# A decoder on one core: the first scan step's inputs in another order, a token shift by transfers, a later turn to tokens

## The chip, the core and the metric

The kernel runs on one core of a Trainium2 chip. A core has five engines with an instruction stream each: TensorE (PE, whose weight loads the profile shows as PEld), VectorE (DVE), ScalarE (ACT), GpSimd (POOL) and SyncE (SP, which issues most transfers here). They work on a common on-chip memory, TensorE writes its results into PSUM, and semaphores order the streams. Within one stream instructions run in the order in which they stand. The metric is the device time of one execution in microseconds.

## The reference

The input `x` is 4 sequences of 512 tokens with 128 features, in float32; a context of 32 tokens for each sequence serves two cross attentions. Six blocks follow each other, each as `x = layernorm(x + block(x))`:

```
x = _layernorm(x + _L0_attn_ref(x, ...))    # selective scan (Mamba), 256 channels, 16 states
x = _layernorm(x + _L0_xattn_ref(x, ...))   # cross attention, 16 heads, gated
x = _layernorm(x + _L0_ffn_ref(x, ...))     # shared + 8 experts, 2 of them for each token
x = _layernorm(x + _L1_attn_ref(x, ...))    # banded self attention, 16 heads of 8
x = _layernorm(x + _L1_xattn_ref(x, ...))   # cross attention, 16 heads
x = _layernorm(x + _L1_ffn_ref(x, ...))     # two layers: local attention, gated feed-forward
```

Three places matter here. In the scan block each sequence goes through a projection, a convolution over four tokens, `silu`, and projections that give `delta = softplus(...)`, `B` and `C`; then `h = exp(delta * A) * h + delta * B * u` runs over the tokens for each of the 16 states, and the result is multiplied by `silu(z)`. In the last block each layer has

```
def shift_token(t):
    t1, t2 = jnp.split(t, 2, axis=-1)
    t2 = jnp.pad(t2, ((0, 0), (1, 0), (0, 0)))[:, :-1]
    return jnp.concatenate([t1, t2], axis=-1)
```

before the attention and again before the feed-forward part: features 64 to 127 come from the token before. After the second shift a layernorm is taken over the features of each token.

## The kernel before

Tokens lie on the 128 partitions, four tiles of 128 tokens a sequence; `T` is 512, `NJ` 4, `B` 4, `NT` 16. All stages stand one after the other in one program. In the parts that matter the order on each engine is written out by hand (`tc.manual_schedule()`): functions are called in the order in which their instructions are to stand in the streams, and the framework adds the waits.

**Front of the scan (L356 to L400).** For sequence 0: squares and their sums give `inv`, the tokens are scaled and turned to features (`xnp`), and the two halves `c` of the 256 channels are projected and convolved, half 0 by four accumulating matmuls with `w_tap` (L375), half 1 by one projection and four DVE instructions (L370, L372) into `acc`. `squares_` of the sequences 1 to 3 stand ahead of that, on ACT and DVE, and `inverses` ahead of half 0's convolution. After the silus (L376, L377), `double` projects to `px` (three copies of B and C, and the step's rank), `rests` takes what bfloat16 drops, `gates` and two silus make `sz`, `steps_` computes softplus in passes `t`, `v`, `w` on ACT, `corrected` and `reduced` mend its rounding, `logarithms` takes the log, `deltas` and `products` give `delta` and `du` (half 0 on POOL, half 1 on DVE), and `parts` completes `stk`, the bfloat16 pieces of B and C.

**The scan (L563 to L598).** 64 steps, state by state for each sequence. Step `k`: `rows` spreads a row of B and one of C over the partitions with a selecting matmul from `stk` (`pb`, `pc`, copied by ACT to `cb`), `decay` makes `dA` on ACT three steps ahead, `scan` multiplies `pb` by `du` (L432), runs the scan (L435) on DVE and multiplies by `cb` on POOL (L440), `collect` sums up on PE. The table `ahead` prepares the next sequence in the gaps; `gates_next` ends with two silus of 1024 columns (L548). `gated` (L450) uses `sz` of a sequence one sequence later.

**Banded attention (L1335 to L1360).** 64 steps `s`, four to a tile `i` of 128 queries. Each step: `scores(s + 1)` (matmuls into `psc`, then the maximum `nm` on DVE), `exponentials(s + 1)` on ACT, `weights(s)` (eight transposes `ptp` and copies to `pT`, one by DVE and one by ACT), `values(s - 1)`. What follows a finished tile is spread over the next steps by

```
tail = [[None, gathered], [by_tokens, None], [by_features, output], [normed, None]]
```

with the first entry of a pair right after `scores` and the second after `values`. `gathered` copies `pa` to `ao` on ACT, `by_tokens` turns it with four transposes `pn` and divides on DVE. `made` prepares the next sequence. `pn`, `pq`, `pto` and `po` share the one buffer of a PSUM tag.

**Last block (L1731 to L1792).** A loop over `g`, two to each tile `i` (four heads each), eight half blocks `q` (two layers, four sequences). `around` and `feed` say which function stands in which of three places of a step; `feed` lags one or two half blocks behind. `output` writes `xa`; `ff_shift` turns `xa` to features (`shifted`: four transposes `pts`, an ACT copy and a DVE copy by one column), one step later `ff_tokens` turns it back (`pth`, ACT copy to `hn`), the step after `ff_stats` takes means and variances, then `ff_norm`, `ff_features`, `ff_gates`, `ff_hidden`, `ff_out`. Functions ask PSUM for buffers of the tag `pt`, of which there are three. `project_v` copies values to `va` and sends them by transfers on SP to `vh`, shifted by 64 partitions. After the loop the last half block (`e`) runs alone.

Of the kernel before, what the change touches and what calls it, by code (L numbers as in the profile page):

```python
# [11 lines left out]
F32 = mybir.dt.float32  # L12
# [45 lines left out]
def decoder_kernel(ctx: ExitStack, tc: tile.TileContext, a: dict):  # L58
# [34 lines left out]
    def vcol(name, i=0):  # L93
        o = _VEC[name][0] + i
        return vec[:, o:o + 1]
# [141 lines left out]
    with ExitStack() as ph:  # L237
# [30 lines left out]
        def squares_(b):  # L268
            sq = fp.tile([P, T], F32, tag="left", name="sq", bufs=1)
            sq = sq.rearrange("p (j d) -> p j d", d=D)  # L270
            S.activation(sq, x0[:, b * NJ:(b + 1) * NJ, :], AF.Square)
            V.tensor_reduce(inv[:, b], sq, AX.X, ALU.add)

        def inverses(lo, hi):
            t = inv[:, lo:hi].rearrange("p b j -> p (b j)")
            V.tensor_scalar(t, t, 1.0 / D, 1e-5, ALU.mult, ALU.add)
            rpow(t, t, (hi - lo) * NJ)
# [17 lines left out]
        def gates(b, c, pi):  # L295
            mm(pi, w_in[:, (2 + c) * P:(3 + c) * P], xnp[:, 3:])
# [18 lines left out]
            G.tensor_tensor(stk[64:96, b, :], left[64:96], mid[64:96], ALU.subtract)  # L315


        def steps_(b, c, pd):
            mm(pd, w_dt[96:104, c * P:(c + 1) * P], xdts[b][96:104])
            t = fp.tile([P, T], F32, tag="e", name="e")  # L320
            v = fp.tile([P, T], F32, tag="v", name="v")
            S.activation(t, pd, AF.Abs, bias=vcol("dt_b", c))
            S.activation(v, pd, AF.Relu, bias=vcol("dt_b", c))
            S.activation(t, t, AF.Exp, scale=-1.0)
            w = fp.tile([P, T], F32, tag="w", name="w")
            S.activation(w, t, AF.Identity, bias=1.0)
            evs[b, c] = t, v, w

        def corrected(b, c):
# [25 lines left out]
        with tc.tile_pool(name="m1ps", bufs=1, space=PSUM) as ps, tc.manual_schedule():  # L355
            squares_(0)  # L356
            inverses(0, 1)
            xns[0] = fp.tile([P, NJ, D], F32, tag="e", name="xn")
            V.tensor_tensor(xns[0], x0[:, 0:NJ, :], inv[:, 0].unsqueeze(2).to_broadcast([P, NJ, D]), ALU.mult)
            by_features(0, ps.tile([P, NJ, P], F32, tag="pt", name="pt"))  # L360
            for c in range(2):
                G.tensor_tensor(w_tap[:, c], w_tap[:, c],
                                w_in[:, c * P:(c + 1) * P].unsqueeze(1).to_broadcast([P, 4, P]), ALU.mult)
            for b in range(1, B):
                squares_(b)

            pi = ps.tile([P, T], F32, tag="pi1", name="pi")
            mm(pi, w_in[:, P:2 * P], xnp[:, 3:])
            acc = u[:, 1, 0, :]
            V.tensor_scalar(acc, pi, vcol("conv_w", 7), vcol("conv_b", 1), ALU.mult, ALU.add)  # L370
            for k in range(1, 4):
                V.scalar_tensor_tensor(acc[:, k:], pi[:, 0:T - k], vcol("conv_w", 7 - k), acc[:, k:], ALU.mult, ALU.add)  # L372
            inverses(1, B)
            pi = ps.tile([P, T], F32, tag="pi0", name="pi")
            convolved(0, 0, pi, range(4))  # L375
            S.activation(u[:, 1, 0, :], acc, AF.Silu)  # L376
            S.activation(u[:, 0, 0, :], pi, AF.Silu, bias=vcol("conv_b", 0))  # L377
            double(0, ps.tile([104, T], F32, tag="px", name="px"))
            rests(0)
            pz = [ps.tile([P, T], F32, tag=f"pz{c}", name="pz") for c in range(2)]  # L380
            for c in range(2):
                gates(0, c, pz[c])
                S.activation(sz[:, c, 0, :], pz[c], AF.Silu)
            S.activation(gate, rcol("gate"), AF.Tanh)
            pct = ps.tile([P, P], F32, tag="pi1", name="pct")
            TE.transpose(pct, ctx_sb, ident)
            V.tensor_copy(ctxT, pct)
            a0 = _VEC["A_log"][0]
            S.activation(negA, vec[:, a0:a0 + 32], AF.Exp)
            V.tensor_scalar_mul(negA, negA, -1.0)  # L390
            V.tensor_scalar_mul(gb, rcol("b_out"), gate)
            for c in range(2):
                steps_(0, c, ps.tile([P, T], F32, tag=f"pd{c}", name="pd"))
                corrected(0, c)
                reduced(0, c, (G, V)[c])
            logarithms(0)
            for c, eng in ((0, G), (1, V)):
                deltas(0, c, eng)
                products(0, c, eng)
            parts(0)  # L400


        with tc.tile_pool(name="m2", bufs=3) as t2, \
# [19 lines left out]

            def decay(k):
                b, n = steps[k]
                for c in range(2):
                    S.activation(dAs[k % 4][:, c, c:T], delta[b % 2][:, c, c:T], AF.Exp,  # L427
                                 scale=negA[:, c * NST + n:c * NST + n + 1])

# [112 lines left out]
            def gates_next(b, c):  # L542
                pi = bank()
                gates(b, c, pi)
                S.copy(sz[:, c, b, :], pi)
                if c:
                    for t in (u, sz):
                        S.activation(t[:, :, b, :], t[:, :, b, :], AF.Silu)  # L548

            def double_next(b):  # L550
                double(b, bank()[0:104])
# [605 lines left out]
    with tc.tile_pool(name="wa", bufs=2) as bp, tc.tile_pool(name="wa_p", bufs=2) as t1, \  # L1157
# [150 lines left out]
        def normed(i):  # L1308
# [4 lines left out]
        made = {3: [(turn_x,)], 5: [(rotary, 0, 0)], 6: [(rotary, 0, 1)], 7: [(rotary, 1, 0)], 9: [(rotary, 1, 1)],  # L1313
                10: [(head_values,)], 11: [(head_keys, 0), (head_keys, 1)], 12: [(head_keys, 2), (head_keys, 3)],
                13: [(head_keys, 4), (head_keys, 5)], 14: [(head_keys, 6), (head_keys, 7)]}
        tail = [[None, gathered], [by_tokens, None], [by_features, output], [normed, None]]

        def tails(s, k):
            i = s // 4 - 1
# [4 lines left out]
        with tc.manual_schedule():  # L1324
            beside = {3: [(blocks_x, 1)], 5: [(g_x, 0)], 6: [(g_x, 1)], 7: [(g_x, 2)], 9: [(g_x, 3)], 10: [(v_x, 0), (v_x, 1)],
                      11: [(v_x, 2)], 12: [(v_x, 3)]}
            blocks_x(0)
            for t in sorted(made):
                for f, *c in made[t]:
                    f(0, *c)  # L1330
                for f, *c in beside.get(t, []):
                    f(*c)
            scores(0)
            exponentials(0)
            last = 4 * NT  # L1335
            for s in range(last):
                if s + 1 < last:
                    scores(s + 1)
                tails(s, 0)
                if s + 1 < last:  # L1340
                    exponentials(s + 1)
                weights(s)

                if s < HT_:
                    for q in range(2):
                        gather(1, 2 * s + q)
                if s % 2 == 0 and 4 <= s < 4 + 2 * HT_:
                    combined(1, s // 2 - 2)
                if s % 2 and 4 <= s < 4 + 2 * HT_:
                    norm_3(1, s // 2 - 2)  # L1350
                if s:
                    values(s - 1)
                tails(s, 1)
                if s // 16 + 1 < B:
                    for f, *c in made.get(s % 16, []):
                        f(s // 16 + 1, *c)
            values(last - 1)
            for s in range(last, last + 4):
                tails(s, 0)
                tails(s, 1)  # L1360

    kept.close()

# [27 lines left out]
    with tc.tile_pool(name="la_b", bufs=2) as bp, tc.tile_pool(name="la_t", bufs=2) as t1, \  # L1391
# [1 line left out]
            tc.tile_pool(name="la_ps", bufs=2, space=PSUM) as ps:  # L1393


        hTz = [bp.tile([P, T], F32, tag=f"hT{k}", name=f"hT{k}", bufs=1) for k in range(3)]
        for k in hTz:
            V.memset(k[64:128, 0:1], 0.0)
        va = bp.tile([P, NJ, 8, 65], F32, tag="va", name="va", bufs=1)
# [5 lines left out]
        ins = [x5]  # L1405
        hTs, pqks, tas, tbs, rns, sss, qTs, pes, pTs, ats, aTs = ({} for _ in range(11))
        xTs, xes, xps, xpTs = ({} for _ in range(4))
        xas, h2s, hns, hnTs, xabs, ges, mvs, fins = ({} for _ in range(8))


        def shift(b):
# [149 lines left out]
            V.tensor_tensor(xas[i // NJ][:, i % NJ, :], po, ins[i // NT][:, i % NT, :], ALU.add)  # L1561

        def ff_shift(q):
            l, b = divmod(q, B)
            xa = xas.pop(q)
            h2s[q] = hTz[2]
            shifted(nc, ps, xa, 0, h2s[q], ident, 3)
            xabs[q] = bp.tile([P, NJ, D], F32, tag="xab", name="xab", bufs=2)
            G.tensor_tensor(xabs[q], xa,
                            rcol("f_b2", 128 * l, 128).unsqueeze(1).to_broadcast([P, NJ, D]), ALU.add)  # L1570
            if l == 1:
                G.tensor_tensor(xabs[q], xabs[q], x5[:, b * NJ:(b + 1) * NJ, :], ALU.add)

        def ff_tokens(q):
            pt = ps.tile([P, NJ, P], F32, tag="pt", name="pth", bufs=3)
            hT = h2s.pop(q)
            for j in range(NJ):
                TE.transpose(pt[:, j, :], hT[:, j * P:(j + 1) * P], ident)
            hns[q] = bp.tile([P, NJ, D], F32, tag="hn", name="hn", bufs=1)
            S.copy(hns[q], pt)  # L1580

        def ff_stats(q):
            mv, rs = stats4(hns[q])
# [114 lines left out]
        def x_norm(b):  # L1698
# [14 lines left out]

        feed = {(0, 0): [[], [], [(ff_hidden, 2, 0)]], (0, 1): [[], [(ff_hidden, 2, 1)], []],
                (1, 0): [[(ff_shift, 1)], [(ff_hidden, 2, 2)], []],
                (1, 1): [[(ff_tokens, 1)], [], []],
                (2, 0): [[(ff_stats, 1)], [(ff_out, 2)], []],
                (2, 1): [[], [], [(ff_norm, 1)]],
                (3, 0): [[(last_stats, 2)], [], []],
# [11 lines left out]
        with tc.manual_schedule():  # L1731
# [46 lines left out]
            ff_shift(e)  # L1778
            for c in range(3):
                ff_hidden(e - 1, c)  # L1780
            ff_tokens(e)
            ff_stats(e)
            ff_out(e - 1)
            ff_norm(e)
# [149 lines left out]
```

## Time and profile before

| | before |
|---|---|
| median of 3 runs | 1281.07 us (1275.3 to 1281.63) |
| profiled execution | 1280.2 us, span 1278.5 us |
| granted TensorE clock, mean | 0.943 |
| busy of the span | PE 86%, DVE 71%, ACT 57%, POOL 50% |
| front, to 38 us | PE 15.5, DVE 13.5, ACT 23.0, POOL 16.9 us busy |
| scan, 38 to 308 us | PE 229, DVE 241, ACT 188, POOL 189 us busy |
| banded attention, 555 to 800 us | PE 217, DVE 165, ACT 140, POOL 43 us busy |
| end, 1230 to 1279 us | PE 31.6, DVE 17.9, ACT 16.6, POOL 8.2 us busy |

A row of the order of time gives start, duration, engine, line and operation, the tiles `out<-in`, the shape and the count; in brackets stands how long the engine was idle before it and which instruction ended that. Rows with a count above 1 are merged, so their duration covers all of them with the gaps. Matmul ends are modelled: the distance between the starts of two groups is TensorE's pitch, and the shown duration of a group is longer than that. L157 and L189 are helpers (`rpow`, `mm`), so their rows are told apart by their tiles.

### The profile page before, as it was taken

The page shows a single profiled execution, that of the slowest core. Times are in us where ns is not written, and L with a number is a line of the kernel's source. Part 1 is how long each engine was busy: PE and PEld are TensorE (multiplying, and loading weights), DVE is VectorE, ACT ScalarE, POOL GpSimd, SP SyncE. Part 2 cuts the span into 40 slices and gives each one's busy share as a digit, 9 for nine tenths or more (in the row PEclk, how much of TensorE's full clock was granted, in tenths as well). Part 3 has the DMA queues.
Part 4 walks back from the last instruction along what each step waited for, and adds up shares of the span by engine and source line. Part 5 has one row for each costly group of instructions (what it writes and reads, how often), then busy time and mean ns, then how long its engine had stood idle before and what let it go on. Part 6 is the DMA issues. An engine that isn't in the chain of part 4 may idle for free.

```text
span 1278.5 us, 22122 instructions
## 1 busy us (share of the span) xinstructions
PE 1100.2 (86%) x8429; PEld 712.8 (56%) x8429; DVE 910.4 (71%) x1722; ACT 729.9 (57%) x1612; POOL 638.2 (50%) x509
## 2 busy tenths in 40 slices
PE   4879888787698789988898998778999999999985
PEld 1334433343366779855555565446666566666563
DVE  3889898897876556847866666687777667766743
ACT  5696958662353445544656565346676665665752
POOL 3568675864546143433110100467785666676621
PEclk9799989897798899989999999899999999999997
DMA  9000000001200612200000000000110100110100
GB/s 270 1 0 1 1 0 1 1 0 65 84 1 30 228 63 80 63 22 14 2 1 2 2 2 2 0 9 21 28 23 14 27 22 15 26 23 14 35 14 17
DMA packets 34573, 38.92 MB, mean 30 GB/s; under 512 B 3378, under 2 KB 25667, under 8 KB 33987
## 3 DMA queue, kind: packets, MB, share of 16 engines
q1 hardware_dynamic: 31874, 31.69, 8.6%
q0 software_dynamic: 2048, 4.20, 1.1%
q10 hardware_dynamic: 544, 1.62, 0.5%
q8 instruction: 66, 1.08, 0.4%
q14 instruction: 41, 0.33, 0.1%
HBM read 20.80 MB, written 9.18 MB: 23 GB/s over the span
## 4 chain that ended last, share of the span: by engine, by line
PE 49%; DVE 16%; ACT 6%; issue 2%; POOL 2%; DMA 0%; DVEq 0%; ACTq 0%; POOLq 0%; SPq 0%
PE psc L189 9%; PE pa L189 4%; PE pqk L189 4%; PE pff L189 3%; PE po L189 3%; PE ptp L1260 3%; PE phg L189 3%; PE pog L189 2%; PE pv L189 2%; PE pof L189 2%; PE ptp L1527 1%; ACT pe L1250 1%; PE ptq L1476 1%; PE pq L189 1%; DVE nm L1243 1%
## 5 line engine op out<-in xcount | busy, mean ns | idle before, releaser
L440 POOL TENSOR_TENSOR h<-h,cb 128x1024 f32<-128x1024 f32 (+1 forms) x65 | 151.8, 2338 | 66.3 <-DVE h L435 49.8
L157 POOL TENSOR_TENSOR rs<-ve,cneg 128x1 f32<-128x1 f32 (+1 forms) x81 | 59.0, 728 | 232.5 <-DVE ve L166 193.8
L435 DVE TENSOR_TENSOR_SCAN h<-dA,pb 128x1024 f32<-128x1024 f32 x64 | 146.4, 2287 | 18.5 <-ACT dA L427 4.9
L1250 ACT ACTIVATE pe<-psc,nm 128x256 f32<-128x256 f32 (+1 forms) x256 | 93.6, 449 | 73.1 <-DVE nm L1243 72.8
L189 PE MATMUL y<-h,ident 128*128 128x512 f32 x256 | 127.2, 620 | 5.4 <-POOL h L440 4.7
L1458 POOL TENSOR_TENSOR ta<-ta,tb 128x1024 f32<-128x1024 f32 x32 | 75.4, 2357 | 111.6 <-DVE rc L1542 65.1
L1243 DVE TENSOR_REDUCE nm<-psc 128x4 f32<-128x1024 f32 (+1 forms) x64 | 69.8, 1091 | 56.7 <-PE psc L189 49.8
L157 POOL TENSOR_TENSOR rn<-ss,cneg 128x16 f32<-128x16 f32 x32 | 93.0, 2906 | 0.0
L1512 DVE TENSOR_REDUCE nm<-psc 128x4 f32<-128x512 f32 x64 | 44.0, 687 | 64.4 <-PE psc L189 62.7
L427 ACT ACTIVATE dA<-delta,negA 128x512 f32<-128x512 f32 (+1 forms) x128 | 85.3, 715 | 4.7 <-POOL delta L346 4.4
L189 PEld LDWEIGHTS y<-h,ident 128*128 128x128 f32 x256 | 49.6, 198 | 65.1 <-issue 46.5
L929 ACT ACTIVATE hTg<-phg,bias 128x128 f32<-128x128 f32 x184 | 52.7, 368 | 57.9 <-PE phg L189 57.2
L432 DVE TENSOR_TENSOR pb<-du,pb 128x1024 f32<-128x1024 f32 x64 | 77.5, 1211 | 2.7 <-PE pb L189 2.2
L1521 ACT ACTIVATE pe<-psc,nm 128x128 f32<-128x128 f32 x256 | 73.8, 381 | 5.4 <-DVE nm L1512 5.3
L189 PE MATMUL pb<-stk,sel 96*128 96x512 bf16 x128 | 41.5, 408 | 32.7 <-DVE h L435 15.5
L1260 PE MATMUL ptp<-ident,pe 128*128 128x128 f32 x448 | 64.5, 281 | 4.8 <-ACT pT L1262 2.0
L189 PE MATMUL pqk<-f_qkv,hT 128*128 128x512 f32 x128 | 64.9, 631 | 4.1 <-DVE tb L1452 4.0
L189 PE MATMUL psc<-kb,qk 64*128 64x256 f32 (+1 forms) x512 | 67.1, 381 | 0.0
L1466 POOL TENSOR_TENSOR ta<-ta,rn 128x1024 f32<-128x1024 f32 x32 | 60.9, 1903 | 2.4
L1260 PEld LDWEIGHTS ptp<-ident,pe 128*128 128x128 f32 x448 | 49.8, 142 | 16.9 <-issue 6.7
L189 PEld LDWEIGHTS <-sel 96*128 96x128 bf16 x192 | 18.9, 103 | 69.3 <-issue 42.3
L1432 ACT ACTIVATE sq<-pqk 128x1024 f32<-128x1024 f32 x32 | 32.9, 1029 | 42.8 <-PE pqk L189 35.3
(375 smaller groups left out, 2879.6 us busy)
## 6 DMA issues: line engine op xcount, KB each, us to landing
vh<-va SPq DMA_DIRECT2D x56, 130.0 KB, 2.3
w<-in_e_w_dram SPq DMA_DIRECT2D x16, 256.0 KB, 5.2
xs<-zero SPq DMA_DIRECT2D x2, 1472.0 KB, 12.7
xg<-xs SPq DMA_DIRECT2D x10, 256.0 KB, 3.1
ys<-yg SPq DMA_DIRECT2D x10, 256.0 KB, 2.4
f_qkv<-in_f_qkv_dram SPq DMA_DIRECT2D x1, 1536.0 KB, 6.6
x<-in_x_dram SPq DMA_DIRECT2D x4, 256.0 KB, 10.8
w_kv<-in_w_kv_dram SPq DMA_DIRECT2D x1, 1024.0 KB, 8.1
```

Of the source, the lines that this page charges most:

```text
L157: G.tensor_tensor(out, in_, cneg.to_broadcast([P, n]), ALU.pow)
L189: TE.matmul(out, lhsT=lhsT, rhs=rhs, start=start, stop=stop)
L427: S.activation(dAs[k % 4][:, c, c:T], delta[b % 2][:, c, c:T], AF.Exp, scale=negA[:, c * NST + n:c * NST + n + 1])
L432: V.tensor_tensor(pb, du[steps[k][0] % 2], pb, ALU.mult)
L435: V.tensor_tensor_scan(h.rearrange("p c t -> p (c t)"), dAs[k % 4].rearrange("p c t -> p (c t)"), pb.rearrange("p c t -> p (c t)"), 0.0, A ...
L440: G.tensor_tensor(h[:, c], h[:, c], cb.unsqueeze(1).to_broadcast([P, n, T]), ALU.mult)
L1243: V.tensor_reduce(nm, psc[:, :, 0:nk], AX.X, ALU.max, negate=True)
L1250: S.activation(pe[:, h, 0:nk], psc[:, h, 0:nk], AF.Exp, bias=nm[:, h:h + 1])
L1260: TE.transpose(ptp[:, h * nb + kk, :], pe[:, 2 * pr + h, kk * P:(kk + 1) * P], ident)
L1458: G.tensor_tensor(ta, ta, tbs.pop(i).rearrange("p w h d -> p (w h) d"), ALU.add)
L1466: G.tensor_tensor(ta, ta, rns.pop(i).unsqueeze(2).to_broadcast([P, 16, 64]), ALU.mult)
L1521: S.activation(pes[g][:, h, :], o[:, par, q, :], AF.Exp, bias=nm[:, k:k + 1])
```

## The change

Four edits. In the front the squares of sequences 1 to 3 move behind the silus of sequence 0; the two passes `v` and `w` of softplus go to DVE; the pieces of `stk` are made right after `px`, two of them on DVE; the gates' projections are copied raw, and their silu is taken in the scan with sequence 1's. `decay` of step 0 takes half 1 ahead of half 0. In banded attention `by_tokens` stands behind `weights` of its step. In the last block `ff_shift` writes `hn` directly: features 0 to 63 by an ACT copy, features 64 to 127 by two transfers on SP that move each token's half to the next partition, and a memset for the first token; `ff_tokens` and the buffer `hT2` go, and `hn` has two buffers.

```diff
-        def steps_(b, c, pd):
+        def steps_(b, c, pd, eng=None):
...
             S.activation(t, pd, AF.Abs, bias=vcol("dt_b", c))
-            S.activation(v, pd, AF.Relu, bias=vcol("dt_b", c))
+            if eng:
+                eng.tensor_scalar(v, pd, vcol("dt_b", c), 0.0, ALU.add, ALU.max)
+            else:
+                S.activation(v, pd, AF.Relu, bias=vcol("dt_b", c))
             S.activation(t, t, AF.Exp, scale=-1.0)
             w = fp.tile([P, T], F32, tag="w", name="w")
-            S.activation(w, t, AF.Identity, bias=1.0)
+            if eng:
+                eng.tensor_scalar_add(w, t, 1.0)
+            else:
+                S.activation(w, t, AF.Identity, bias=1.0)
...
-            for b in range(1, B):
-                squares_(b)
...
-            inverses(1, B)
             pi = ps.tile([P, T], F32, tag="pi0", name="pi")
             convolved(0, 0, pi, range(4))
+            squares_(1)
             S.activation(u[:, 1, 0, :], acc, AF.Silu)
             S.activation(u[:, 0, 0, :], pi, AF.Silu, bias=vcol("conv_b", 0))
+            squares_(2)
+            squares_(3)
+            inverses(1, B)
             double(0, ps.tile([104, T], F32, tag="px", name="px"))
-            rests(0)
-            pz = [ps.tile([P, T], F32, tag=f"pz{c}", name="pz") for c in range(2)]
-            for c in range(2):
-                gates(0, c, pz[c])
-                S.activation(sz[:, c, 0, :], pz[c], AF.Silu)
+            left = fp.tile([P, T], F32, tag="left", name="left", bufs=1)[0:96]
+            V.tensor_tensor(left, xdts[0][0:96], stk[:, 0, :], ALU.subtract)
+            mid = fp.tile([96, T], BF16, tag="mid", name="mid", bufs=1)
+            V.tensor_copy(mid[64:96], left[64:96])
+            V.tensor_copy(stk[32:64, 0, :], left[32:64])
+            G.tensor_tensor(stk[64:96, 0, :], left[64:96], mid[64:96], ALU.subtract)
...
             for c in range(2):
-                steps_(0, c, ps.tile([P, T], F32, tag=f"pd{c}", name="pd"))
+                steps_(0, c, ps.tile([P, T], F32, tag=f"pd{c}", name="pd"), V)
                 corrected(0, c)
                 reduced(0, c, (G, V)[c])
+            for c in range(2):
+                pz = ps.tile([P, T], F32, tag=f"pz{c}", name="pz")
+                gates(0, c, pz)
+                V.tensor_copy(sz[:, c, 0, :], pz)
             logarithms(0)
             for c, eng in ((0, G), (1, V)):
                 deltas(0, c, eng)
                 products(0, c, eng)
-            parts(0)
...
             def decay(k):
                 b, n = steps[k]
-                for c in range(2):
+                for c in range(2) if k else (1, 0):
...
                 if c:
-                    for t in (u, sz):
-                        S.activation(t[:, :, b, :], t[:, :, b, :], AF.Silu)
+                    for t, i in ((u, b), (sz, b)) + ((sz, 0),) * (b == 1):
+                        S.activation(t[:, :, i, :], t[:, :, i, :], AF.Silu)
...
-        tail = [[None, gathered], [by_tokens, None], [by_features, output], [normed, None]]
+        tail = [[None, None, gathered], [None, by_tokens, None], [by_features, None, output], [normed, None, None]]
...
                 weights(s)
+                tails(s, 1)
...
                     values(s - 1)
-                tails(s, 1)
+                tails(s, 2)
...
         def ff_shift(q):
+
             l, b = divmod(q, B)
             xa = xas.pop(q)
-            h2s[q] = hTz[2]
-            shifted(nc, ps, xa, 0, h2s[q], ident, 3)
+            hn = hns[q] = bp.tile([P, NJ, D], F32, tag="hn", name="hn", bufs=2)
+            nc.sync.dma_start(hn[1:P, :, 64:D], xa[0:P - 1, :, 64:D])
+            nc.sync.dma_start(hn[0:1, 1:NJ, 64:D], xa[P - 1:P, 0:NJ - 1, 64:D])
+            G.memset(hn[0:1, 0, 64:D], 0.0)
+            S.copy(hn[:, :, 0:64], xa[:, :, 0:64])
...
-        def ff_tokens(q):
-            pt = ps.tile([P, NJ, P], F32, tag="pt", name="pth", bufs=3)
-            hT = h2s.pop(q)
-            for j in range(NJ):
-                TE.transpose(pt[:, j, :], hT[:, j * P:(j + 1) * P], ident)
-            hns[q] = bp.tile([P, NJ, D], F32, tag="hn", name="hn", bufs=1)
-            S.copy(hns[q], pt)
...
-                (1, 1): [[(ff_tokens, 1)], [], []],
```

Line numbers in the text are those of the kernel before, unless it says otherwise.

## The prediction

> **What bounds the kernel now.** I read the chain that ended last, the busy time by stretches, the order of time where the change cuts in, and the DMA packets. By the page the chain is mostly TensorE:
>
> ```profile
> PE 49%; DVE 16%; ACT 6%; issue 2%; POOL 2%; DMA 0%; DVEq 0%; ACTq 0%; POOLq 0%; SPq 0%
> ```
>
> The stretches (columns: length, then busy us of PE, PEld, DVE, ACT, POOL, granted clock, DMA share, GB/s) separate the stages: the scan is DVE's (241 of 270 us), banded attention PE's with gaps (217 of 245), the last stage PE's nearly without gaps (48 of 50).
>
> ```profile
> 38.00:308.00 270.00, 229.02 (x704) 105.86 (x702) 241.40 (x186) 188.16 (x336) 189.32 (x97) 0.94 0.00 1
> 555.00:800.00 245.00, 216.83 (x2302) 141.83 (x2300) 164.59 (x345) 139.84 (x372) 42.76 (x61) 0.98 0.02 6
> 1050.00:1100.00 50.00, 47.66 (x479) 32.03 (x480) 34.84 (x72) 31.22 (x68) 32.15 (x17) 1.00 0.11 25
> ```
>
> So a shorter front moves the scan forward whole, and PE time or PE waits taken out later count whole, until something else is late.
>
> **Front (L364 to L400).** The order of time:
>
> ```profile
> 15.10 0.80 DVE L370 TENSOR_SCALAR u<-pi,vec 128x512 f32<-128x512 f32 x1
> ...
> 25.39 0.67 ACT L322 ACTIVATE e<-pd,vec 128x512 f32<-128x512 f32 x1
> ...
> 36.77 1.01 PE L189 MATMUL pb<-stk,sel 96*128 96x512 bf16 x2 [11.53 <-POOL stk L315]
> ...
> 37.88 1.23 DVE L432 TENSOR_TENSOR pb<-du,pb 128x1024 f32<-128x1024 f32 x1 [2.17 <-PE pb L189]
> ```
>
> The first scan step's multiply starts at 37.88 behind a late `stk`. Now: DVE has its convolution input at 11.63 but stood behind three reductions until 15.18; with those behind, `acc` is ready at about 15. The other half waits for PE's convolution (17.04), so its silu ends at 17.8 instead of 19.49, and `px` at 19.8 instead of 21.5. Two squares fall into the gap. The gates' two silus (1.2) leave ACT, so L322 starts at 22.6 instead of 25.39. Its softplus halves from eight passes (0.6 each) to four: the second Exp ends at 25.2 instead of 29.5. DVE takes over two bias-and-max from PSUM (0.80, as L370), two adds (0.43, as L1215), two `left` pieces (0.4 by the same row), two gate copies (0.69 as L387's kind at this width) and keeps its own. POOL has the later blocks' `inv` power (2.28, now asked for at 20.8) until 23.1 and then its piece of `stk` (1.48 at L315). From `left` at 21.1 DVE's order is: pieces to 22.5, small ones to 23.2, first pair to 25.1 (0.80+0.43+0.69), second to 27.1, `reduced` to 28.5, copies to 29.9, delta 30.6, product 31.4. `stk` is whole by 24.6, PE's `pb` long before. The multiply starts at about 31.4: 6.4 gained. Bounds: L346 took 1.40 beside POOL and 0.69 is its price alone (L342); if all SBUF-only operations here pay the double, 3 are lost; with none, 0.5 more is won.
>
> One silu of 128x1024 (1.04, L548) moves into the scan, and ACT isn't free there: behind L548 the scan at 75.23 waits 3.10 us, released by ACT's `cb`. So it costs its 1.0. `decay` only swaps two instructions of 0.63; free. Front: -5.4 (-2.4 to -5.9).
>
> **Turn to tokens (L1284).** Who waits for `ao` (us, times), and one place:
>
> ```profile
>   PE pn L1288: 12.0, 13
> ```
> ```profile
> 657.38 0.66 PE L1288 MATMUL pn<-ident,ao 128*128 128x128 f32 x4 [0.96 <-ACT ao L1280]
> ```
>
> PE stands 0.92 each time with eight `ptp` transposes ready behind it. After, these go first (PE is free at 656.42, `pe` done at 656.4), and `ao` (done 657.33) is there when `pn` comes: the whole 12.0 could go. DVE now copies `pT` (0.68) before it reads `pn`, so `pn`'s bank (`ps`, one buffer) comes free at 659.0, and `pq`, where L1313 puts one next (6 of the 16), waits for it: 0.4 kept of 0.95. 12.0 - 6 x 0.55 = 8.7, I take 8.5 (3 to 12; 3 if the other steps too run into DVE's `nm`).
>
> **Shift by transfers (L1563 to L1580).** Per half block eight transposes, two ACT copies (0.58, 0.59) and a DVE copy (0.69) go; an ACT copy from SBUF (0.4, by L1262's 128x256), a one-row memset on POOL and two SP transfers come.
>
> ```profile
> 1066.09 0.33 PE L1799 MATMUL pts<-ident,xa 128*128 128x128 f32 x1 [0.36 <-DVE xa L1561]
> 1066.26 0.60 PE L1527 MATMUL ptp<-ident,pe 128*128 128x128 f32 x4
> ...
> 1072.73 0.60 PE L1578 MATMUL pth<-ident,hT 128*128 128x128 f32 x4
> ...
> 1078.06 0.28 DVE L176 BATCH_NORM_STATS2 st<-hn 128x6 f32<-128x128 f32 x1
> ```
>
> PE's saving is its pitch: `pts` from 1065.19 to `ptp` at 1066.26, 1.07 with the wait for `xa`; `pth` 0.43. That is 1.5, seven times in the loop: 10.5.
>
> Against it stands the landing. The transfer moves 127 rows of four 256-byte pieces, 508 packets. The DMA queue's rows (packets, MB, share of 16 engines) in the windows 0:60, 1076:1081 and 1272:1278.5:
>
> ```profile
> q1 hardware_dynamic: 9378, 7.01, 39.6%
> ```
> ```profile
> q1 hardware_dynamic: 80, 0.13, 12.5%
> ```
> ```profile
> q1 hardware_dynamic: 528, 0.26, 13.5%
> ```
>
> The second is one `vh` transfer: 64 rows and 16 closing packets, one for each engine. Adding up the first window by rows, 9378 comes out only if `w_dt` (8 rows) closes 8 times and `b2all` (9 rows) 9 times; with 16 closings each it is 9393. So the number of engines follows the row count, and every transfer that spread over 16 had a multiple of 16 rows. 127 divides by nothing: I take one engine. Its time: `vh` costs 12.5% x 16 x 5.0 = 10.0 us over 64 rows, 156 ns for 2080 bytes; by bytes 256 cost 19 ns, 508 cost 9.8 us. The third row, 512-byte packets, gives 13.5% x 16 x 6.5 / 528 = 26.6 ns; by packets 13.5 us. `vh` lands after 2.3 us with four rows an engine (0.6), so 1.7 is fixed: landing 11.5 to 15.2, I take the middle, 13.3. Spread over 16 engines it would be `vh`'s 2.3.
>
> The Trainium skill has the rule (DMA: Bandwidth & Descriptors, section "Why a DMA increments its semaphore by 16 and not by 1"): a transfer from SP runs on the largest number up to 16 that divides its slowest dimension, and it names 127 partitions as one engine. By it the sum is the forecast's; without it, the first rival's.
>
> In the loop `xa` is done at 1066.04 and DVE's statistics want `hn` 12.0 later, 10.5 once PE is faster. Behind L176 on DVE stand the `kT` copy (ends 1080.53, wanted by `psc` at 1083.72) and `at` (wanted 1.8 after, plus 0.76 that DVE idled before it): 2.5 of slack. So 13.0 is free and 13.3 costs 0.3, against 1.5: 7 x -1.2 = -8.4 (-10.5 at 11.5, +4.9 at 15.2). On SP the pair waits for `xa` after the `vh` issues of 1064.35 and 1064.90; the next, of 1076.08, queues behind it on the engine and is wanted two blocks on. ACT's copy waits for `xa` with `pT` and `qT` behind it, but ACT reached this place 2.1 us before its data until now. The memset's buffer is free since two half blocks.
>
> At the end nothing covers it:
>
> ```profile
> 1245.04 0.29 DVE L1561 TENSOR_TENSOR xa<-po,y 128x128 f32<-128x128 f32 x1 [3.25 <-PE po L189]
> ...
> 1250.56 0.29 DVE L176 BATCH_NORM_STATS2 st<-hn 128x6 f32<-128x128 f32 x1 [0.36 <-ACT hn L1580]
> ```
>
> All that follows waits for these statistics: 1245.4 + 13.3 against 1250.56 is +8.1 (6.3 to 10.0; -0.8 if spread, where DVE's own L1617 holds). Shift: -0.3 (-4.2 to +14.9; -11.3 if spread).
>
> **Sum.** -5.4 - 8.5 - 0.3 = -14.2 against the profiled execution's 1280.2 (span 1278.5 and 1.7 around it): 1266.0. The median of before is 0.9 higher, within its runs' own spread. What a measurement can tell from no change is 0.5%, 6.4 us.
>
> **Rivals.** *The transfer spreads over 16 engines:* 1280.2 - 5.4 - 8.5 - 11.3 = 1255. For it: all big transfers so far spread. Against: the 8- and 9-row ones. 0.18.
>
> *Slower: DVE stands at L176 for one overloaded engine.* With landing L the shift costs 7 x (L - 13.0 - 1.5) + L - 5.2. It eats all 13.9 of the rest at L = 15.1 and is 0.5% slower from 15.9. At 30 ns a packet L is 17: +29.3, 1296. For it: a lone engine has been timed on no small piece here. Against: 512 bytes took 26.6 ns. 0.10.
>
> *The turn's wait only moves* to `pm` and DVE, 3 gained: 1271.5. For it: banded attention's chain passes through `nm` and `pe`. 0.10.
>
> *The forecast,* 1266, 0.62; its own range (L from 11.5 to 14.6) is 1258 to 1276. Of it 0.53 lies below 1274.7, 0.08 within 0.5%, 0.01 above. With the first rival whole and 0.06 of the last, faster is 0.77; the last's rest gives same 0.12; the second and 0.01 slower 0.11. For 8 in 10 the range takes in most of the spread case and the slow one's beginning: 1251 to 1284.
>
> **What would show it.** First L432-type multiply at 31 to 32, the scan waiting about 4 us once at its eighth step. `pn` without an idle PE before it, `pq` waiting on `at` instead. Transfers to `hn` landing 11 to 15 us after issue; in the loop DVE idle at L176 for 1 to 5 us; at the end some 8 us of DVE wait. A landing under 4 us, or one over 16, breaks the shift's sum; a first multiply after 34 the front's.

## The result, and the profile after

After the change the median of six runs is 1259.55 us (1256.39 to 1264.54), against 1278.92 us of six runs of before: a ratio of 0.9853, 95% interval 0.9822 to 0.9884. The profiled execution took 1256.39 us, its span is 1254.7 us, its mean granted clock 0.951 (before: 1280.2, 1278.5 and 0.943). The forecast was 1266.0 us, with a range of 1251 to 1284.

The chain that ended last, of after (shares of the span). DMA has 2%, where before had 0%: of its 23.5 us 18.4 are two `hn` transfers, that of the loop's first half block and that of the end.

```profile
PE 43%; DVE 18%; issue 6%; ACT 3%; POOL 3%; DMA 2%; DVEq 0%; ACTq 0%; POOLq 0%; SPq 0%
```

The same three stages of after in the busy time by stretches, moved forward by 7, 8 and 10 us (columns as before: length, busy us of PE, PEld, DVE, ACT, POOL, clock, DMA share, GB/s). The second changed most: in banded attention's window stand 222.5 us of TensorE work in 243 us, where 216.8 in 245 stood.

```profile
31.00:301.00 270.00, 224.99 (x692) 104.18 (x691) 239.61 (x186) 190.05 (x339) 186.29 (x95) 0.94 0.00 1
547.00:790.00 243.00, 222.52 (x2301) 142.49 (x2300) 164.25 (x346) 139.71 (x372) 42.92 (x62) 0.97 0.02 6
1040.00:1090.00 50.00, 48.20 (x493) 31.95 (x492) 35.84 (x72) 32.25 (x73) 31.16 (x17) 1.00 0.10 23
```

**Front.** After, in order of time around the first scan step, without weight loads. The first multiply (L443, before L432) starts at 30.82, not at 37.88. But the first decays (L438, before L427) start at 30.00, and they had started at 35.20: they are only 5.2 earlier, because they now wait for `delta`, which stands on VectorE behind two gate copies (L407).

```profile
28.69 0.67 DVE L407 COPY sz<-pz 128x512 f32<-128x512 f32 x1
29.29 0.67 DVE L352 TENSOR_TENSOR delta<-v,w 128x512 f32<-128x512 f32 x1
...
29.51 1.01 PE L189 MATMUL pb<-stk,sel 96*128 96x512 bf16 x2 [6.34 <-DVE sz L407]
...
30.82 1.23 DVE L443 TENSOR_TENSOR pb<-du,pb 128x1024 f32<-128x1024 f32 x1
```

The decays themselves are six, ahead of the first `cb` on ScalarE, in before (first line) and after (second):

```profile
35.20 3.78 ACT L427 ACTIVATE dA<-delta,negA 128x512 f32<-128x512 f32 x6
```
```profile
30.00 3.78 ACT L438 ACTIVATE dA<-delta,negA 128x511 f32<-128x511 f32 x6 [1.54 <-DVE delta L352]
```

So TensorE stands at the second `pc` until ScalarE has copied the first one to `cb`, 0.44 us in before (first line) and 2.50 in after (second), and all that follows in its stream with it:

```profile
39.50 0.58 PE L189 MATMUL pc<-stk,sel 96*128 96x512 bf16 x1 [0.44 <-ACT cb L422]
```
```profile
34.30 0.59 PE L189 MATMUL pc<-stk,sel 96*128 96x512 bf16 x1 [2.50 <-ACT cb L433]
```

Behind it the scan's steps 3 to 7 (counted from 0) wait 3.4 us together, where before had 1.5. With the longer silu, step 9 waits 4.85 us (second line) where before had 3.10 (first; this step is the one that the prediction calls the eighth and an expectation the ninth):

```profile
75.23 2.29 DVE L435 TENSOR_TENSOR_SCAN h<-dA,pb 128x1024 f32<-128x1024 f32 x1 [3.10 <-ACT cb L422]
```
```profile
71.80 2.29 DVE L446 TENSOR_TENSOR_SCAN h<-dA,pb 128x1024 f32<-128x1024 f32 x1 [4.85 <-PE y L189]
```

The scan of step 0 is 7.05 us earlier than in before, that of step 4 5.5, of step 9 3.4, the last (300.52 against 303.22) 2.7.

**Turn.** Of the waits of TensorE in banded attention (us, times, longest), `pn` for `ao` has fallen from 12.0 us in 13 to one, and six waits of `pq` have come, for `at`, which reads the bank after `pn`:

```profile
PE pq L189 <- DVE at L1304: 2.2, 6, 0.5
...
PE pn L1299 <- ACT ao L1291: 0.7, 1, 0.7
```

**Shift.** The end of after: the transfer (L1580) is issued when `xa` is done, and the statistics start 9.23 us later (called the landing below), after 6.19 us in which VectorE waited for nothing else. In the loop it waited for a transfer once, 0.9 us in the last half block.

```profile
1216.25 0.29 DVE L1573 TENSOR_TENSOR xa<-po,y 128x128 f32<-128x128 f32 x1 [2.96 <-PE po L189]
...
1216.60 0.73 SPq L1580 DMA_DIRECT2D hn<-xa  x1
...
1217.39 6.43 SPq L1581 DMA_DIRECT2D hn<-xa  x1
...
1225.83 0.29 DVE L176 BATCH_NORM_STATS2 st<-hn 128x6 f32<-128x128 f32 x1 [6.19 <-DMA hn<-xa]
```

The transfers of after in the window 1216:1228, 40 slices of 0.3 us. While the `hn` pieces run, the core moves an even 15 to 19 GB/s (21 in one slice): a piece of 256 bytes every 14 ns.

```profile
GB/s 287 92 58 0 0 0 8 15 15 15 15 17 17 18 18 18 19 18 18 18 19 18 18 18 19 18 18 18 21 18 18 6 0 0 0 0 0 0 0 0
```

How many engines carry it shows in the packets of 1217.9 to 1226 (first line), where these transfers run alone, and of the same place in the kernel with the transfer cut into 112 and 15 rows, 1230.1 to 1233 (second; this kernel comes below). If each engine closes with one packet, as the prediction counts, 515 are 508 and 3 pieces and 1 + 3 closings, and 545 are 508 and 3 pieces and 16 + 15 + 3 closings. The halved pieces below leave only this split: their 1024 packets are 1016 and 3 pieces and 1 + 1 + 3 closings. So 127 rows went over one engine, and the small transfer of three pieces over three.

```profile
DMA packets 515, 0.13 MB, mean 16 GB/s; under 512 B 515, under 2 KB 515, under 8 KB 515
```
```profile
DMA packets 545, 0.13 MB, mean 45 GB/s; under 512 B 545, under 2 KB 545, under 8 KB 545
```

### The profile page after: what moved, and what is told of

The parts are those of the page before. It is cut to its first block, busy times and chain, and to the rows that moved or that the text cites. A ratio compares the mean times of both kernels' runs of the same rounds, so it can differ in the third digit from the quotient of the medians.

```text
span 1254.7 us, 22047 instructions
## 1 busy us (share of the span) xinstructions
PE 1084.6 (86%) x8365; PEld 697.4 (56%) x8365; DVE 906.8 (72%) x1721; ACT 720.1 (57%) x1597; POOL 638.8 (51%) x517
## 4 chain that ended last, share of the span: by engine, by line
PE 43%; DVE 18%; issue 6%; ACT 3%; POOL 3%; DMA 2%; DVEq 0%; ACTq 0%; POOLq 0%; SPq 0%
PE psc L189 9%; PE pqk L189 4%; PE pa L189 4%; PE ptp L1271 3%; PE pff L189 3%; PE po L189 2%; PE pog L189 2%; PE phg L189 2%; DVE tb L1464 2%; PE pv L189 2%; DVE ss L1450 2%; DVE ta L1457 2%; POOL xs L829 2%; PE pof L189 1%; DMA hn<-xa 1%
## 5 line engine op out<-in xcount | busy, mean ns | idle before, releaser
L438 ACT ACTIVATE dA<-delta,negA 128x511 f32<-128x511 f32 (+1 forms) x128 | 85.3, 715 | 6.3 <-POOL delta L352 4.4
L443 DVE TENSOR_TENSOR pb<-du,pb 128x1024 f32<-128x1024 f32 x64 | 77.5, 1211 | 1.8 <-POOL du L355 1.5
L189 PE MATMUL pff<-hnT,f_w 128*128 128x512 f32 (+1 forms) x96 | 49.7, 638 | 9.8 <-DVE tb L1464 7.3
```

What stands on the lines that cost most here:

```text
L189: TE.matmul(out, lhsT=lhsT, rhs=rhs, start=start, stop=stop)
L443: V.tensor_tensor(pb, du[steps[k][0] % 2], pb, ALU.mult)
```

## The experiments

Ratios hold within one job only: the median of before was 1278.9, 1284.7, 1291.7 and 1286.1 us in the four jobs.

### Each part alone

**The front's edits alone** (the diff's hunks up to `gates_next`).

> Before with the front's edits alone (order of the first scan step's inputs, softplus shared, first gates' silu within the scan). Theory A, the forecast's sum: first multiply near 31, scan 5.4 us earlier to its end, so 1278.9 - 5.4 = 1273.5. Theory B, read from the trace of after: the first scan starts 7.05 us earlier, but the waits at scans 3 to 9 give 4.3 us back, so the last scan is 2.7 us earlier: 1276.2. Theory C: the further 5.7 us that after gained between 312 and 548 us, where nothing is edited, also come from the front: 1270.5, and the first psc(kb) product then comes some 8 us earlier than in the profile of before; by A and B that stretch differs only as the granted clock does.

Measured: ratio 0.9986 (0.9958 to 1.0015), that is -1.8 us (-5.4 to +1.9). First multiply 30.7, last scan 300.2, first `psc<-kb` 556.4. Theory B fits; A lies at the interval's edge and its "scan 5.4 us earlier to its end" is wrong in the trace (the last scan is 3.0 earlier); C falls.

**The turn's edit alone** (`tail`, `tails` and the loop that calls it).

> Before with the turn's edit alone (pn a few instructions later on TensorE). Theory A, the forecast's: -8.5, so 1270.4; pn's waits for ao (12.0 us, 13 times) are gone and six of some 0.5 stand before pq. Rival: the wait only moves to pm and VectorE, -3: 1275.9.

Measured: 0.9949 (0.9929 to 0.9968), -6.6 us (-4.1 to -9.1). The profile has the same two waits as after (`pn` for `ao` once, 0.7 us; `pq` for `at` six times, 2.2 us). The forecast's theory holds; -3 is outside.

**The shift alone** (`ff_shift`, no `ff_tokens`).

> Before with the shift by transfers alone. Theory A, the forecast's: landing 13.3 us on one DMA engine, loop -8.4, end +8.1: 1278.6. Theory B, from the trace of after: one DMA engine, but 14 ns for a 256-byte piece (18 GB/s while it runs), landing 9.2 us; loop -10.5 to -11.3, end +4.1: 1271.7 to 1272.5. If instead the loop's gain in after owed something to the other two edits, the time stays within 3 us of before, 1276 or more.

Measured: 0.9968 (0.9954 to 0.9983), -4.1 us (-2.2 to -5.9). The transfer was issued at 1240.22 and the statistics started at 1249.46, so the landing is 9.24 again. From the first `psc<-kT` to the last `xa` the loop took 361.9 us; in three kernels without the edit it took 372.8, 373.1 and 371.7. Theory B in kind; its end was -6.4 to -7.2, a little beyond the interval.

### After once more, and what varies

**After itself, in two later jobs.** The second was the mark for the last two kernels below.

> After itself, unchanged, in one job with the three kernels below. Its first profile reached the first psc(kb) product at 547.8 us, while the kernel with the front alone, the same to there, reached it at 556.4 and the one with the cut transfer at 559.0. Theory B: 5.7 to 11 us of the 23.8 between the two profiles of before and after are the granted clock's from run to run and no part of the change: psc(kb) first at 553 to 558 here, and the time 1.2 to 1.5% below before. Rival: the gain belongs to the whole change, and psc(kb) comes at 548 again.

> After itself once more, as the mark for the two kernels below in the same job: 1.2 to 1.5% below before, last scan at 300.2 to 300.5 us.

Measured: 0.9856 (0.9818 to 0.9893) and 0.9881 (0.9849 to 0.9913). The first `psc<-kb` came at 557.0 and 560.9, not at 547.8. From the first `sc` to that product, where nothing is edited, the first profile of after took 235.8 us, before 241.5, and the eleven kernels run later 242.5 to 246.9. What differs most is the granted clock (the column behind the busy times), here of after (first line) and of the front alone (second). Both run the same program here and stand within four TensorE instructions of each other at 460 us; in the next 30 us after gets through 248, the other through 202:

```profile
460.00:490.00 30.00, 28.48 (x248) 27.41 (x247) 14.98 (x26) 12.88 (x46) 7.57 (x9) 1.00 0.28 84
```
```profile
460.00:490.00 30.00, 26.71 (x202) 25.59 (x202) 13.29 (x23) 10.27 (x36) 7.02 (x8) 0.89 0.25 74
```

Over 400 to 550 us it was 0.97 in that profile, and 0.92 to 0.95 in the rest. The clock is not the whole of it. In the eleven later kernels TensorE also stands 0.8 to 2.5 us of this stretch for nothing that the profile names ("issue"), in the first profiles of before and after not at all. In the front alone two of these waits come some 8 us before its clock falls:

```profile
464.16 0.51 PE L189 MATMUL po<-w2s,hT 128*128 128x128 f32 x3 [0.91 <-issue]
465.59 0.83 PE L189 MATMUL po<-w2s,hT 128*128 128x128 f32 x6 [0.92 <-issue]
```

So 5.8 of the 23.8 us between the two first profiles (that stretch's difference) are not the change's.

### The landing

**The transfer cut into 112 and 15 rows.**

```diff
-            nc.sync.dma_start(hn[1:P, :, 64:D], xa[0:P - 1, :, 64:D])
+            nc.sync.dma_start(hn[1:113, :, 64:D], xa[0:112, :, 64:D])
+            nc.sync.dma_start(hn[113:P, :, 64:D], xa[112:P - 1, :, 64:D])
```

> After with the 127-row transfer cut into 112 rows and 15 rows. Theory B (the landing is long because 508 pieces stand in line on one DMA engine): the 112 rows go over 16 engines and the 15 over 15, and from the first issue to the statistics at the end go about 4 us instead of 9.2; in the loop next to nothing is won, since VectorE waited there only 0.9 us once; at the end 5 us: 1259.5 - 5 to -6, about 1254. Rival: the landing is mostly a fixed price of a transfer out of and into SBUF, whatever the engines: then it stays at 9 us, the third issue on SyncE adds 0.8, and the time is 1259.5 to 1261.

Measured: 0.9818 (0.9792 to 0.9843), a lower ratio than any of after's, though not in the same job and with intervals that overlap. The trace says where. Its view of the tile `hn` gives the landings of this kernel:

```profile
DMA to landing us min/median/max: 2.1/2.2/2.4
```

No wait of VectorE for a transfer is left. At the end the statistics start 3.03 us after the first issue, right behind VectorE's own work:

```profile
1228.89 0.66 SPq L1580 DMA_DIRECT2D hn<-xa  x1
...
1231.92 0.29 DVE L176 BATCH_NORM_STATS2 st<-hn 128x6 f32<-128x128 f32 x1
```

From the last `xa` to the span's end 31.7 us pass; in after and five kernels with the same transfer 37.0 to 38.4, in three without 32.6 to 33.4. The loop takes 361.5 us, as in after. Theory B holds in its mechanism and in its place. The closing packets, 1 for 127 rows and 16 and 15 for the cut, agree with the rule that the prediction cites; the Trainium skill's rule (DMA: Bandwidth & Descriptors, section "Why a DMA increments its semaphore by 16 and not by 1") gives 16 engines for 112 rows and 15 for 15.

**Pieces of half the size.**

```diff
-            nc.sync.dma_start(hn[1:P, :, 64:D], xa[0:P - 1, :, 64:D])
+            for lo in (64, 96):
+                nc.sync.dma_start(hn[1:P, :, lo:lo + 32], xa[0:P - 1, :, lo:lo + 32])
```

> After with each 256-byte piece of the 127-row transfer sent as two of 128 bytes (two transfers, 1016 pieces). If a piece costs its 14 ns whatever its length, the landing goes from 9.2 to 16.3 us (17 with the second issue); past the forecast's slack of 13.0 us that costs 3.3 to 4 us in each of seven half blocks and 7 to 8 at the end: 30 to 36 us above after. If the price goes by bytes, the landing stays near 10 and the time within 2 us of after. If the landing doubles but the loop has more slack than 13.0, only the end's 7 to 8 us show.

Measured: 0.9896 (0.986 to 0.9932), after in the same job 0.9856 (0.9818 to 0.9893): some 5 us more by the middle, with intervals that overlap. The trace is clearer. The end and the last half block of the loop:

```profile
1244.70 0.29 DVE L176 BATCH_NORM_STATS2 st<-hn 128x6 f32<-128x128 f32 x1 [8.40 <-DMA hn<-xa]
```
```profile
1212.74 0.29 DVE L176 BATCH_NORM_STATS2 st<-hn 128x6 f32<-128x128 f32 x1 [3.00 <-DMA hn<-xa]
```

The landing is 11.4 us (1233.26 to 1244.70), not 16.3 and not 10. So neither branch was right: taking off 1.8 us as fixed (an estimate: 2.2 us of the cut transfer less its 28 pieces an engine), a 256-byte piece takes 14.6 ns and one of 128 bytes 9.5 ns. About 4.4 ns of a piece go to no byte, if its price is a fixed part and one by bytes; the second issue is in this too. At a landing of 11.4 VectorE waits in all seven half blocks of the loop: 1.0 us in the first, 0.2 to 0.4 in five, 3.0 in the last. The loop takes 364.3 us, 2.8 more, 0.9 of it in the first half block and 1.8 in the last. So the statistics are wanted 8.4 to 11.1 us after the issue, not everywhere alike.

### The scan's give-back

**Without the first gates' silu.**

```diff
-                    for t, i in ((u, b), (sz, b)) + ((sz, 0),) * (b == 1):
+                    for t, i in ((u, b), (sz, b)):
```

> After without the silu of the first sequence's gates (left out of the computation; in after it stands in the scan beside the two of the second sequence). Theory B: ScalarE's table episode is 1.0 us shorter, the ninth scan's wait falls from 4.85 to some 3.1, and the last scan comes 1.7 us earlier; the other 2.6 us that the scan gave back remain, since they come from ScalarE's first decays, which start only 5.2 us earlier and not 7.05. Rival: all of the 4.3 us is the silu's, and the last scan comes 4 us earlier. In the time neither is more than 0.3%.

The result then lacks the silu of the first sequence's gates. Measured: 0.9841 (0.9799 to 0.9882), last scan 297.8 (after in the same job 300.2). Step 9's wait is now for `dA`:

```profile
69.39 2.29 DVE L446 TENSOR_TENSOR_SCAN h<-dA,pb 128x1024 f32<-128x1024 f32 x1 [2.35 <-ACT dA L438]
```

The silu costs 2.4 us instead of the 1.0 of the forecast or the 1.7 expected: it ends one wait (4.78 there) and leaves 2.35. The rest of the give-back stays, against the rival.

**The gate copies on ScalarE**, with the cut transfer.

```diff
+            pz = [ps.tile([P, T], F32, tag=f"pz{c}", name="pz") for c in range(2)]
             for c in range(2):
-                pz = ps.tile([P, T], F32, tag=f"pz{c}", name="pz")
-                gates(0, c, pz)
-                V.tensor_copy(sz[:, c, 0, :], pz)
-            logarithms(0)
+                gates(0, c, pz[c])
+            for c in range(2):
+                w = wvs[0, c][0]
+                S.activation(w, w, AF.Ln)
+                S.copy(sz[:, c, 0, :], pz[c])
```

> After with the transfer cut into 112 and 15 rows, and the two gate copies (1.27 us on VectorE ahead of delta) put on ScalarE between and behind the two logarithms, where it stood 0.78 and 1.54 us. Theory B: delta at 28.1 instead of 29.3, first multiply at 29.6 instead of 30.8, the first decays at 29.0 instead of 30.0 and with them TensorE's queue behind cb: 1.0 us; the end 6 us shorter than in after: 7 us below after, some 1 below the kernel with the cut alone. Rival: the copies only delay the last table load as much as they free VectorE: first decays still at 30, nothing gained on the cut transfer.

Measured: 0.983 (0.9789 to 0.9871), which can't be told from the cut alone (its loop took 364.0 us, 15.4 instead of 13.4 of them after the last `psc<-kT`, with the granted clock at 0.85 there). First multiply 30.54, first decays 29.71: only 0.1 to 0.3 gained of 1.2. VectorE reached `delta` at 28.11 as expected, but the instruction took 1.57 us instead of 0.67, next to GpSimd's product of the other half:

```profile
28.11 1.57 DVE L352 TENSOR_TENSOR delta<-v,w 128x512 f32<-128x512 f32 x1
```
```profile
27.54 1.59 POOL L355 TENSOR_TENSOR du<-delta,u 128x512 f32<-128x512 f32 x1
```

GpSimd's ends at 29.13, VectorE's 0.55 later. The rival's "nothing gained" was nearly right, its cause (the table load) wrong: that load ends at 28.77, before either of these. The Trainium skill (SBUF — State Buffer, section "Who interferes with whom") has a lock of this kind, between a VectorE instruction with two inputs in SBUF and a GpSimd instruction that reads SBUF; these two lines agree with it.

**The scan's start in another order.**

```diff
-                for k in range(3):
-                    decay(k)
                 for k in range(2):
+                    decay(k)
                     rows(k)
                 unit(1)
                 turn_next(1)
+                decay(2)
```

> After with the start of the scan in another order: ScalarE makes each of the first two decays and then that step's cb, turns the second sequence, and makes the third decay last; in after all three decays (3.78 us) stand ahead of the first cb. Theory B (the scan's steps 3 to 8 wait for TensorE, whose queue stands behind pc until ScalarE has copied cb, and ScalarE's decays began only 5.2 us earlier): cb and TensorE's convolutions come 1.7 us earlier, the waits of 0.6 to 0.9 at steps 3 to 7 go for the most part, and the last scan is at 298.5 instead of 300.2. Rival (TensorE's low clock at the stage's beginning is what costs, and it lasts to a fixed time): convolutions earlier but as much slower, last scan at 300. The time differs by 0.13% at most.

Measured: 0.9878 (0.9843 to 0.9912), the time no different from after's 0.9881 in the job, as expected. In the trace the second `pc` waits no more, the steps 3 to 5 run without a wait, and from the first scan to the last it takes 264.8 us. In after in the same job it is 269.3 (268.1 to 269.5 in seven kernels with this front), without the front's edits 263.2 to 264.0. So 4.6 us are back, nearly all that had been given back, and more than the 1.7 of theory B, because step 9's wait shrinks as well. The last scan starts at 297.7, so the rival with its 300 is out:

```profile
68.58 2.29 DVE L446 TENSOR_TENSOR_SCAN h<-dA,pb 128x1024 f32<-128x1024 f32 x1 [3.30 <-ACT dA L438]
```

**Both, as the best version.**

> The same order at the scan's start, and the transfer cut into 112 and 15 rows. Theory B: 1.7 from the scan and 6 from the end: 7.7 us or 0.6% below after in the same job, with the statistics at the end about 3.5 us behind xa instead of 9.6. Rival: the third transfer's issue and contention in the loop eat what the end gains, within 2 us of after.

Measured: 0.98 (0.9774 to 0.9825), median 1257.82 us against 1270.79 of after and 1286.09 of before in the same job. The interval lies whole below after's (0.9849 to 0.9913). In the trace 4.6 us come from the scan and 7.3 from the end (30.8 us instead of 38.2); the statistics start 3.4 us after the start of the last `xa`. This is the lowest ratio found here; the cut alone, at 0.9818 (0.9792 to 0.9843) in another job, can't be told from it by the time.

## Why the prediction was right, and where its steps were not

The time by stages, of all thirteen profiles (us; the front's row is a point of time, the others are lengths). A kernel stands under "with" where it holds the edit in the form of after, for the first multiply in any form:

| stage | without the edit | with it | difference | forecast |
|---|---|---|---|---|
| first multiply of the scan | 37.3 to 37.9 (3 kernels) | 30.5 to 31.7 (10) | -6.5 | -6.4 |
| first scan to last scan | 263.2 to 264.0 (3) | 268.1 to 269.5 (7) | +5.0 | +1.0 |
| first `psc<-kb` to last `pn` | 238.7 to 243.4 (3) | 230.4 to 237.8 (10) | -7.8 | -8.5 |
| first `psc<-kT` to last `xa` | 371.7 to 373.1 (3) | 361.4 to 362.1 (6) | -10.9 | -8.4 |
| last `xa` to the end | 32.6 to 33.4 (3) | 37.0 to 38.4 (6) | +5.0 | +8.1 |

The differences are those of the means. Their sum is -15.2, the forecast's -14.2; the measured ratio makes -18.8 (-14.8 to -22.8). The first profile of after shows -23.8: 5.8 of that lie between 312 and 548 us, where its clock was better, and the rest of the gap is that it stands at the good end of several rows. The forecast's mechanism stood, and its total came close with the help of errors that cancel, which is luck.

**The front's term was right for the multiply and wrong for what follows.** The working listed VectorE's order op by op and came within 0.6 us. The step that failed is "a shorter front moves the scan forward whole": it took the multiply as the only thing that the scan waits for. Two streams feed it. ScalarE's decays moved by 5.2 only, those of three steps ahead of the first `cb`, and TensorE stood behind that; the kernel with another order shows it by undoing it. The silu was priced at its own 1.04, "so it costs its 1.0"; it stands in an episode for which scan and TensorE wait in turn, and cost 2.4 in the kernel that leaves it out.

**The turn's term was right,** its waits too: 0.7 us left at `pn`, six new waits of `pq` behind `at`, and the kernel with it alone at -6.6 (-4.1 to -9.1). The rival in which the wait only moves is out.

**The shift's term was mis-sized: the landing.** One engine, as forecast, but 9.2 us instead of 13.3, below the lower bound of 11.5. The price of a piece was taken from `vh`'s bytes and from 512-byte packets (19 to 27 ns for a piece); alone on its engine a piece takes 14 to 15. Both prices were sums of packet times, and those overlap on one engine: from 1218.2 to 1225.2 in after, the 485 packets add up to 8.7 us (7.8% of 16 engines over 7.0 us), 18 ns each, while one starts every 14.4.

```profile
DMA packets 485, 0.12 MB, mean 18 GB/s; under 512 B 485, under 2 KB 485, under 8 KB 485
...
q1 hardware_dynamic: 485, 0.12, 7.8%
```

So the loop paid almost nothing, and the end 5.0 instead of 8.1; of the 5.0, 4.3 lie ahead of the statistics and 0.7 behind them. The loop's -10.9 is not all the shift's. To the last `psc<-kT` the kernels with the edit gain 9.4 us (348.1 to 348.6 against 357.6 to 357.7), or 1.3 of the 1.5 forecast for a half block. The other 1.4 or so lie behind that, where the clock was 0.85 to 0.94 in the three kernels without the edit and 0.96 to 1.00 in the six with it. The kernel with the gate copies on ScalarE has the edit too and took 15.4 us there at 0.85, as long as before, so this part goes with the clock. The two errors together are 5.6 us in the change's favour, these 1.4 included, and the front's is 3.9 against it (-6.5 + 5.0 against -5.4).

**The slack in the loop was read from one half block.** The working took that one for all seven and had 13.0 us free. In after the statistics of the five middle half blocks start 11.0 us behind the issue without a wait, and those of the first 10.4; with the cut transfer those of the last start at 8.3. When the halved pieces landed at 11.4, the five waited 0.2 to 0.4 us and took no longer, which fits the working; but 1.0 of wait cost the first 0.9, and 3.0 cost the last 1.8. With a landing of 9.2 this cost nothing to speak of. At the 13.3 of the forecast, by the same points (an estimate), it would have cost some 2.8 us in the first and 3.7 in the last, not 0.3 each; so the slower rival began nearer than the text says.

**The rival that spreads over 16 engines** did not happen in after. Made by hand, it brings what was forecast of it at the end: the stretch after the last `xa` is 31.7 and 30.8 us with the cut, 1.7 and 2.6 below before (forecast -0.8).

**What stays open:** what sets the granted clock from run to run (0.943 to 0.951 in after's runs, which are 1264.5 and 1256.4 us); and whether the parts add up exactly. Multiplied, the three alone give 0.9903, after gave 0.9853 to 0.9881 in other jobs, and their intervals are too wide to call that a difference.

## What to carry to other kernels

When a stage is fed by several in-order streams, work out for each of them when it arrives, not only for the one that was last: the gain is at most that of the stream that moved least, and a queue behind one small copy can take most of it (here 2.7 us were left of 7). A transfer that replaces a computation has a landing that the loop hides and the end does not; count its rows before writing it, since cutting 127 rows into 112 and 15 took some 7 us off the end here. A sum of packet times is not the time of a line of packets, since the packets of one engine overlap. And compare stages over several profiles before reading a difference of a few us as the change's: one profile had 6 us that no other had, and the loop's last stretch was 2 us longer where the clock was lower.

## What the runs showed of the hardware

- A transfer of 127 rows of four 256-byte pieces within SBUF closed with one packet, ran at 18 GB/s and landed after 9.2 us; 112 rows and 15 rows closed with 16 and 15 and landed after 2.2. The small transfer behind the 127 rows held SyncE for 6.4 us in its issue, and 0.74 us behind the cut ones, so here a long line on one engine held the issuing stream too.
- Halving the pieces to 128 bytes raised the landing to 11.4 us, not to twice: about 14.6 and 9.5 ns for a piece, by estimate. The 256-byte packets took 18 ns each by the records and began every 14.4.
- TensorE's granted clock at the scan's beginning stays at 0.50 for 2 to 4 us after its work has become dense (no idle time in windows of 2 us): to 40 us in after, where that began at 36, to 46 in before, where it began at 42, and to 38 in the kernel with the other order, where it began by 36. The low stretch moved with the work.
- An addition of two SBUF inputs on VectorE took 1.57 us beside a GpSimd product and 0.67 alone.
